# A decoder layer on one core: early context loads, and routers of two tiles in the two halves of the array

## The chip, the core and the metric

The kernel runs on one core of a Trainium2 chip. The core has TensorE (matmuls, PE in the profile; PEld is its loading of weights), VectorE (DVE), ScalarE (ACT), GpSimd (POOL) and SyncE (SP), which here only issues DMAs. [...] The metric is device microseconds of the whole program; less is better. All data is float32.

## What is computed

One decoder layer over x of shape 32 x 64 x 512, that is 2048 tokens of 512 features, in 16 tiles of 128 tokens. Three residual steps, each on a layernorm of x:

```
x = x + attention(layernorm(x))          # 32 heads of 128, RMS norm of q and k, sequences of 64
x = x + cross_attention(layernorm(x), ctx_1024)
x = x + experts(layernorm(x))

# experts, for flat tokens of 512 features, 64 experts, the best 8
logits   = flat @ router_weight.T + router_bias
scores   = softmax(logits)
w_dense  = scores where among the 8 largest of its token, else 0
out      = flat * w_dense.sum(-1) + w_dense @ expert_bias
```

In the cross attention the attention runs over features: for a batch entry, 512 features attend to 128 context features over the 64 positions; a skip product with a 64 x 64 matrix is added.

## The kernel before

The program has two stages. The first, up to about 1360 us, makes queries, keys and values of all heads and mixes them; mixed heads go to DRAM as `mixed`. The second, the output stage, multiplies the mixed heads with the output weights and runs cross attention and experts for each tile. Both parts of the change are in the second.

**The output products.** Tiles are taken in pairs: pair k has tiles 2k and 2k + 1. `first_out` does pair 0 while the last attention units finish, `strassen_out` the pairs 1 to 7. A pair is seven products (Strassen's scheme over two tiles and two halves of the features). A product is a PSUM block `py` of 128 x 256, made in four chunks of four matmuls each (`chunks`, L879). The generator yields after each chunk, so a pair has 28 chunks. At its start `strassen_out` loads the pair's mixtures a12, a22, a11, a21 (1 MB each, L863) and the residual tiles (256 KB each, L176), and has POOL add the output bias to them (L867). VectorE makes sums of the mixtures for later products (L1051, L1053, L1058, L1065; 128 x 2048 each) and adds the products to the residual tiles.

**The tails.** When a pair is done, `start_tail` puts a generator for each of its two tiles, `after_attention`, into a list. After each chunk of the next pair, `advance` lets each tail run on if the number of chunks that it asked to wait (its `yield n`) is over. So the cross attention and the experts of pair k are issued between the chunks of pair k + 1. For an even tile, counted in chunks from its first step: layernorm and the load of its context `ct` (step 0), keys (2), scores `e` and softmax (4), transposes of the probabilities into `att` (10), mixing `py_x` and the second layernorm (13), transposes of the router's input `pt_f` and their copy `ft` (17), router `pl` (19). The odd tile does these at 1, 3, 7, 13, 16, 20 and 22.

**The router** (`experts`). Four matmuls (K = 128 features each) have the 128 tokens' features as weights and the 64 columns of the router's matrix `rwt` moving, and leave logits `pl` with tokens in partitions (L1173). VectorE then works on 128 x 64 tiles: it adds the bias (L1178), finds the 8 largest (L1180) and the negated maximum (L1182); ScalarE makes the exponentials and their sum (L1185); VectorE makes the reciprocal (L1187), marks the chosen (L1190, L1192), makes the weights `wds` (L1201) and their sum (L1203), and adds the weighted input to the residual tile (L1205). The even tile ends there and keeps its weights in one half of `wds`; the odd tile, at step 26, has TensorE transpose both tiles' weights at once (`pw`, L1212), ScalarE copy them (`wt`, L1214), and at step 28 TensorE multiply with the expert biases (`pm`, L1222) in two row halves; L1225 adds them and L1226 stores the tiles. Tiles 14 and 15 run `alone`, each by itself.

**The order of work.** TensorE's instructions run in the order in which the program text issues them, everywhere. In the output stage (after `ordered.close()`, L1549) the other engines and the DMA queues are ordered by the compiler's scheduler, each engine in one queue; it also puts in the semaphores. Buffers are by tag: a tile with the same `tag` takes one of `bufs` places in turn and waits until the last reader of that place is through. The pool `output` is opened at L1551 in the memory that the pool of the attention stage left. `ps_a`, `ps_s` and `ps_t` are PSUM pools of 3, 3 and 2 banks. The first pair's order around the change:

```
work = ctx.enter_context(tc.tile_pool(name="output", bufs=2, reuse_waits="tile"))
bo_b = work.tile([P, D], F32, tag="bo", name="bo_b", bufs=1)
load(bo_b, bo.partition_broadcast(P))
outs = {1: strassen_out(1, right, start_tail, a12)}
next(outs[1])
```

Pair 1 issues six chunks, a transpose of two small matrices, one step of the tails, and so on; its mixture a12 is loaded earlier, in `drain`. The contexts of tiles 0 and 1 are loaded at L1090 in the first step of their tails.

Of the kernel before, what the change touches and what calls it, by code (L numbers as in the profile page):

```python
# [27 lines left out]
MCTX = 128  # L28
NEXP = 64
# [12 lines left out]
def decoder_layer(  # L42
# [23 lines left out]
    nc = tc.nc  # L66
# [3 lines left out]
    small = ctx.enter_context(tc.tile_pool(name="small", bufs=4))  # L70
# [5 lines left out]
    ps_a = ctx.enter_context(tc.tile_pool(name="ps_a", bufs=3, space=bass.MemoryType.PSUM))  # L76
    ps_t = ctx.enter_context(tc.tile_pool(name="ps_t", bufs=2, space=bass.MemoryType.PSUM))
    ps_s = ctx.enter_context(tc.tile_pool(name="ps_s", bufs=3, space=bass.MemoryType.PSUM))
# [136 lines left out]
    def load(to, what):  # L215

        tc.keep_in_program_order(nc.sync.dma_start(out=to, in_=what))
# [27 lines left out]
    def fill_behind(t, what):  # L245
        if (t, what) in FILL:
            fill(FILL[t, what])
# [726 lines left out]
    def strassen_out(pair, right, done, a12=None):  # L974
# [106 lines left out]
        done(ta, xa)  # L1081
        done(tb, xb)

    def cross_attention(t, xt, apart):

        name = f"x{t}"
        ct = work.tile([P, MCTX], F32, tag="ct", name=f"ct_{t}")
        nc.sync.dma_start(out=ct, in_=ctx_flat[bass.ts(t, P), :])  # L1090
        xn = layernorm(xt, name)
        yield 1
        kv = ps_s.tile([P, 2, MCTX], F32, tag="ps", name=f"kv_{t}")
        nc.tensor.matmul(kv[:, 0, :], wqk, ct, start=True, stop=True)
        nc.tensor.matmul(kv[:, 1, :], ct, xw[:, 2, :], start=True, stop=True)

        kvs = work.tile([P, 2, MCTX], F32, tag="kvs", name=f"kvs_{t}")
        nc.scalar.copy(kvs, kv)
        fill_behind(t, "keys")
        yield apart  # L1100
        halves = [slice(b * SEQ, (b + 1) * SEQ) for b in range(2)]
        e = [ps_s.tile([P, 4, MCTX], F32, tag="ps", name=f"e{b}_{name}") for b in range(2)]
        for c in range(4):
            for b, half in enumerate(halves):
                nc.tensor.matmul(  # L1105
                    e[b][:, c, :],
                    xn[half, bass.ts(c, P)],
                    kvs[half, 0, :],
                    start=True,
                    stop=True,  # L1110
                )
        def skip():
            py = ps_a.tile([P, D], F32, tag="pa", name=f"py_{name}")
            nc.tensor.matmul(py, xw[:, 3, :], xn, start=True, stop=False, skip_group_check=True)  # L1114
            return py


        py = skip() if t == NT - 1 else None
        probs = []
        for b in range(2):  # L1120

            mx = small.tile([P, 4], F32, tag="mx4", name=f"mx{b}_{name}")
            nc.vector.tensor_reduce(mx, e[b], AX.X, ALU.max)
            neg = small.tile([P, 4], F32, tag="neg4", name=f"neg{b}_{name}")
            nc.vector.tensor_scalar(neg, mx, -(SEQ**-0.5), None, ALU.mult)
            prob = work.tile([P, 4, P], F32, tag="probx", name=f"prob{b}_{name}", bufs=3)
            sums = small.tile([P, 4], F32, tag="sums4", name=f"sums{b}_{name}")
            for c in range(4):
                nc.scalar.activation(
                    prob[:, c, :],  # L1130
                    e[b][:, c, :],
                    AF.Exp,
                    bias=neg[:, c : c + 1],
                    scale=SEQ**-0.5,
                    accum_out=sums[:, c : c + 1],
                )
            inv = small.tile([P, 4], F32, tag="inv4", name=f"inv{b}_{name}")
            nc.vector.reciprocal(inv, sums)
            nc.vector.tensor_tensor(prob, prob, _bc(inv, P), ALU.mult)
            probs.append(prob)  # L1140
        yield 5
        att = work.tile([P, 2, 4, P], F32, tag="att", name=f"att_{name}", bufs=1)
        for b in range(2):
            nc.scalar.copy(att[:, b, :, :], transposed(probs[b], f"{name}_{b}"))
        fill_behind(t, "probabilities")
        yield 2
        py = py or skip()
        for b, half in enumerate(halves):
            nc.tensor.matmul(  # L1149
                py[half, :],  # L1150
                kvs[:, 1, half],
                att[:, b, :, :].rearrange("m c n -> m (c n)"),
                start=False,
                stop=b == 1,
                skip_group_check=True,
            )
        fill_behind(t, "mixtures")
        nc.vector.tensor_tensor(xt, xt, py, ALU.add)
# [3 lines left out]
    def experts(t, xt):  # L1162
        name = f"f{t}"
        xn = layernorm(xt, name)

        yield 8 if t == NT - 2 else 3
        ft = work.tile([P, KC, P], F32, tag="ft", name=f"ft_{name}", bufs=1)
        nc.scalar.copy(ft, transposed(xn.rearrange("p (kc k) -> p kc k", k=P), name))
        fill_behind(t, "router's input")
        yield 1  # L1170
        pl = ps_s.tile([P, NEXP], F32, tag="ps", name=f"pl_{name}")
        for kc in range(KC):
            nc.tensor.matmul(  # L1173
                pl, ft[:, kc, :], rwt[:, kc, :], start=kc == 0, stop=kc == KC - 1
            )
        fill_behind(t, "router")
        lg = work.tile([P, NEXP], F32, tag="lg", name=f"lg_{name}")
        nc.vector.tensor_tensor(lg, pl, rb_b, ALU.add)  # L1178
        top = small.tile([P, 8], F32, tag="top", name=f"top_{name}")
        nc.vector.max(top, lg)  # L1180
        neg = small.tile([P, 1], F32, tag="neg", name=f"neg_{name}")
        nc.vector.tensor_scalar(neg, top[:, 0:1], -1.0, None, ALU.mult)  # L1182
        ex = work.tile([P, NEXP], F32, tag="ex", name=f"ex_{name}")
        den = small.tile([P, 1], F32, tag="den", name=f"den_{name}")
        nc.scalar.activation(ex, lg, AF.Exp, bias=neg, accum_out=den)  # L1185
        inv = small.tile([P, 1], F32, tag="inv1", name=f"inv1_{name}")
        nc.vector.reciprocal(inv, den)  # L1187

        rest = work.tile([P, NEXP], F32, tag="rest", name=f"rest_{name}")
        nc.vector.match_replace(rest, top, lg, -3e38)  # L1190
        chosen = work.tile([P, NEXP], F32, tag="chosen", name=f"chosen_{name}")
        nc.vector.tensor_tensor(chosen, lg, rest, ALU.not_equal)  # L1192

        alone = t >= NT - 2
        side = 0 if alone else t % 2
        if side:
            wds, other = chosen_by.pop(t - 1)
        else:
            wds = work.tile([P, 2, NEXP], F32, tag="wds", name=f"wds_{name}")
        wd = wds[:, side, :]  # L1200
        nc.vector.scalar_tensor_tensor(wd, ex, inv, chosen, ALU.mult, ALU.mult)  # L1201
        ws = small.tile([P, 1], F32, tag="ws", name=f"ws_{name}")
        nc.vector.tensor_reduce(ws, wd, AX.X, ALU.add)  # L1203

        nc.vector.scalar_tensor_tensor(xt, xn, ws, xt, ALU.mult, ALU.add)  # L1205
        if not alone and not side:
            chosen_by[t] = wds, xt
            return
        yield 3
        n = NEXP if alone else 2 * NEXP  # L1210
        pw = ps_t.tile([P, P], F32, tag="pt", name=f"pw_{name}")
        nc.tensor.transpose(pw[0:n, :], wds.rearrange("p a e -> p (a e)")[:, 0:n], ident)  # L1212
        wt = work.tile([P, P], F32, tag="wt", name=f"wt_{name}")
        nc.scalar.copy(wt[0:n, :], pw[0:n, :])  # L1214
        fill_behind(t, "weights")
        yield 1

        both = [(t, xt)] if alone else [(t - 1, other), (t, xt)]
        pms = [ps_a.tile([P, D], F32, tag="pa", name=f"pm{i}_{name}") for i in range(len(both))]
        for i, pm in enumerate(pms):  # L1220
            rows = slice(i * NEXP, (i + 1) * NEXP)
            nc.tensor.matmul(pm, wt[rows, :], eb_sb[rows, :], start=True, stop=True)  # L1222
        fill_behind(t, "experts")
        for (at, it), pm in zip(both, pms):
            nc.vector.tensor_tensor(it, it, pm, ALU.add)  # L1225
            nc.sync.dma_start(out=out_flat[bass.ts(at, P), :], in_=it)  # L1226

# [323 lines left out]
    work = ctx.enter_context(tc.tile_pool(name="output", bufs=2, reuse_waits="tile"))  # L1551
    bo_b = work.tile([P, D], F32, tag="bo", name="bo_b", bufs=1)
    load(bo_b, bo.partition_broadcast(P))
    outs = {1: strassen_out(1, right, start_tail, a12)}
    next(outs[1])

# [88 lines left out]
```

## Time and profile before

| | |
|---|---|
| median of 3 runs | 1869.87 us (1869.63 to 1870.72) |
| the profiled execution | 1869.75 us |
| its span, first to last instruction | 1868.0 us |
| granted TensorE clock | 0.999 |
| instructions | 40676 |

Where the time of the changed parts stands in the groups of the output stage:

| line | what | count | busy us | mean ns |
|---|---|---|---|---|
| L1173 | router matmuls, 128x64 moving | 128 records | 16.2 | 270 |
| L1105 | scores of the cross attention, 64*128, 128x128 | 256 records | 19.1 | 285 |
| L1149 | mixing of the cross attention, 128*64, 128x512 | 64 records | 17.3 | 618 |
| L1094 | keys, 128x128 | 32 records | 6.2 | 276 |
| L1205 | residual of the experts, 128x512 | 16 | 12.0 | 748 |
| L1185 | exponentials of the router, 128x64 | 16 | 5.6 | 348 |

How to read it: a float32 matmul shows as two records, a transpose as one. Records overlap, so a group's cost on TensorE is read from start to start in a timeline or from the chain of waits, not from its busy time. `128*64` ahead of a form is the part of the array that is used: 128 rows (the contraction) by 64 columns; two matmuls in different halves can be in the array together. In a timeline the columns are start, duration (both us), engine, line, operation, output and inputs, count, and in brackets the idle time before and what ended it.

### The profile page before, as it was taken

The page shows a single profiled execution, that of the slowest core. Times are in us where ns is not written, and L with a number is a line of the kernel's source. Part 1 is how long each engine was busy: PE and PEld are TensorE (multiplying, and loading weights), DVE is VectorE, ACT ScalarE, POOL GpSimd, SP SyncE. Part 2 cuts the span into 40 slices and gives each one's busy share as a digit, 9 for nine tenths or more (in the row PEclk, how much of TensorE's full clock was granted, in tenths as well). Part 3 has the DMA queues.
Part 4 walks back from the last instruction along what each step waited for, and adds up shares of the span by engine and source line. Part 5 has one row for each costly group of instructions (what it writes and reads, how often), then busy time and mean ns, then how long its engine had stood idle before and what let it go on. Part 6 is the DMA issues. An engine that isn't in the chain of part 4 may idle for free.

```text
span 1868.0 us, 40676 instructions
## 1 busy us (share of the span) xinstructions
PE 1850.4 (99%) x16914; PEld 1616.9 (87%) x16914; DVE 1245.1 (67%) x2110; ACT 653.6 (35%) x1577; POOL 1014.7 (54%) x852
## 2 busy tenths in 40 slices
PE   9999999999999999999999999999999999999999
PEld 8888998898899888898889988988888888788876
DVE  6877777777666758777667767766684445554555
ACT  2344444444433443434443343444312202221222
POOL 4866777776667639776667777766242121212120
PEclk9999999999999999999999999999999999999999
DMA  4234434433443343333343333334944231223100
GB/s 143 69 122 144 134 125 131 131 109 110 131 136 114 114 139 112 109 109 103 130 134 123 109 110 114 103 115 141 312 122 159 91 116 68 71 94 116 46 26 23
DMA packets 164650, 215.06 MB, mean 115 GB/s; under 512 B 10161, under 2 KB 135153, under 8 KB 160369
## 3 DMA queue, kind: packets, MB, share of 16 engines
q1 hardware_dynamic: 157648, 206.62, 34.2%
q10 hardware_dynamic: 6816, 5.83, 1.0%
q8 instruction: 133, 2.18, 0.5%
q14 instruction: 53, 0.43, 0.1%
HBM read 172.05 MB, written 40.37 MB: 114 GB/s over the span
## 4 chain that ended last, share of the span: by engine, by line
PE 88%; DVE 4%; DMA 3%; POOL 3%; ACT 1%; issue 1%; SPq 0%; ACTq 0%; POOLq 0%; DVEq 0%
PE p_w L685 32%; PE py L879 17%; PE va L417 11%; PE vb L417 8%; PE o L622 3%; PE s L585 3%; PE ms_w L821 3%; PE pt_p L279 1%; PE pa L475 1%; PE e_x L1105 1%; PE py_x L1149 1%; PE pt_x L279 1%; POOL w L120 1%; PE pl_f L1173 1%; PE py_x L1114 1%; PE pb L475 1%
## 5 line engine op out<-in xcount | busy, mean ns | idle before, releaser
L685 PE MATMUL p_w<-x,w 128*128 128x256 f32 x2940 | 721.1, 382 | 2.5 <-DVE qk L696 1.7
L685 PEld LDWEIGHTS p_w<-x,w 128*128 128x128 f32 x2940 | 521.4, 190 | 59.3 <-DVE qk L696 1.2
L417 PEld LDWEIGHTS va<-w,x 128*128 128x128 f32 x2048 | 268.6, 192 | 13.0
L696 DVE TENSOR_TENSOR qk<-p_w,qk 128x512 f32<-128x512 f32 x360 | 213.1, 599 | 94.6 <-PE p_w L685 92.3
L433 ACT COPY v<-va 128x256 f32<-128x256 f32 x256 | 96.2, 376 | 497.5 <-PE va L417 497.5
L417 PE MATMUL va<-w,x 128*128 128x128 f32 x2048 | 269.9, 275 | 0.0
L709 DVE TENSOR_TENSOR qk<-p_w,qk 128x512 f32<-128x512 f32 x360 | 220.5, 620 | 46.5 <-PE p_w L685 43.1
L120 POOL TENSOR_TENSOR w<-w 128x768 f32<-128x768 f32 x126 | 249.7, 1993 | 2.4
L572 POOL TENSOR_TENSOR qk<-qk,rs 128x512 f32<-128x512 f32 x128 | 173.0, 1352 | 111.8 <-DMA rs<-row_w 99.4
L295 POOL TENSOR_TENSOR prob<-prob,inv 128x512 f32<-128x512 f32 x64 | 79.2, 1237 | 281.5 <-DVE inv L294 278.3
L879 PE MATMUL py<-wo,a 128*128 128x256 f32 x992 | 227.2, 382 | 0.0
L386 ACT ACTIVATE sq<-qk 128x512 f32<-128x512 f32 x256 | 161.4, 631 | 183.6 <-DVE qk L709 64.4
L879 PEld LDWEIGHTS py<-wo,a 128*128 128x128 f32 x992 | 184.1, 190 | 32.9 <-issue 8.6
L417 PEld LDWEIGHTS vb<-w,x 128*128 128x128 f32 x1536 | 201.3, 192 | 9.7
L417 PE MATMUL vb<-w,x 128*128 128x128 f32 x1536 | 202.4, 275 | 0.0
L574 DVE SCALAR_TENSOR_TENSOR qk<-qk,gqk,rs 128x512 f32<-128x512 f32 x128 | 164.7, 1287 | 3.8 <-DMA rs<-row_w 3.5
L879 PE MATMUL py<-wo_t,a 128*128 128x256 f32 x672 | 155.1, 382 | 0.0
L879 PEld LDWEIGHTS py<-wo_t,a 128*128 128x128 f32 x672 | 124.3, 190 | 18.2 <-issue 1.6
L1003 POOL TENSOR_TENSOR x<-x,p 128x256 f32<-128x256 f32 x42 | 42.9, 1043 | 166.7 <-ACT p L1056 72.2
L437 DVE TENSOR_TENSOR v<-vb,v 128x256 f32<-128x256 f32 x192 | 80.9, 421 | 57.0 <-ACT v L433 28.8
L765 POOL TENSOR_TENSOR qk<-qk 128x256 f32<-128x256 f32 x120 | 102.8, 857 | 10.5 <-DVE qk L709 5.8
L287 DVE TENSOR_REDUCE mx<-s 128x8 f32<-128x512 f32 x64 | 44.1, 689 | 85.4 <-PE s L585 85.3
(197 smaller groups left out, 2253.7 us busy)
## 6 DMA issues: line engine op xcount, KB each, us to landing
rs<-row_w SPq DMA_DIRECT2D x120, 512.0 KB
mixed<-ot SPq DMA_DIRECT2D x64, 512.0 KB
a<-mixed SPq DMA_DIRECT2D x32, 1024.0 KB
w<-in_wq_dram SPq DMA_DIRECT2D x64, 256.0 KB
w<-in_wk_dram SPq DMA_DIRECT2D x62, 256.0 KB
w<-in_wv_dram SPq DMA_DIRECT2D x62, 256.0 KB
x<-in_x_dram SPq DMA_DIRECT2D x20, 256.0 KB
rs<-row SPq DMA_DIRECT2D x8, 512.0 KB
```

The lines of the kernel that those rows point to most:

```text
L120: on.tensor_tensor(*(it.rearrange("p c j d -> p (c j) d") for it in (out, a, b)), ALU.subtract)
L386: nc.scalar.activation(sq, of, AF.Square)
L417: nc.tensor.matmul(to[:, j, :], left[i][:, c, j, :], right[i][:, c, 2, :], start=first and j == 0 and c == 0, stop=c == 1, skip_group_chec ...
L433: nc.scalar.copy(self.v[h, ab], what)
L437: nc.vector.tensor_tensor(it, what, it, ALU.add)
L572: nc.gpsimd.tensor_tensor(k, k, rk, ALU.mult)
L574: lambda: nc.vector.scalar_tensor_tensor(q, q, gqk, rq, ALU.mult, ALU.mult)
L685: nc.tensor.matmul(bank[:, s, :], self.w.inner[o][i], inner_x[self.half, o][i], start=first and s == 0, stop=True, skip_group_check=True,)
L696: nc.vector.tensor_tensor(to(t, j), bank, add(t, j), ALU.add)
L709: nc.vector.tensor_tensor(to(t, j), bank, to(t, j), ALU.add)
L765: on.tensor_tensor(to, to, what, ALU.add)
L879: nc.tensor.matmul(py, a[:, g, :], b[g // KH][:, g % KH, :], start=n == 0 and g == 0, stop=n == last and g == NHG - 1,)
```

## The change

Two parts. The contexts of tiles 0 and 1 get their tiles and loads in front of `strassen_out(1, ...)`, so ahead of the loads of pair 1's mixtures; `cross_attention` takes them from the dictionary `contexts`, and loads the context itself for all other tiles, as before.

For tiles 0 to 13 the router runs once for both tiles of a pair, at the odd tile's step. The even tile copies its transposed input into one half of `fts` (in the buffer tagged `att`, 128 x 1024) and returns; the odd tile fills the other half. The router's matrix (128 x 64) is now the weights and the 128 tokens move; even and odd tile write partitions 0 to 63 and 64 to 127 of one bank, `plt`, in turn for each of the four parts of the contraction. ScalarE copies this to SBUF (`lgt`); one chunk later TensorE transposes it, so that tokens are in partitions again, and VectorE adds the bias for both tiles in one operation. The operations from the maximum to the residual then run for the two tiles one after the other in the program text. The wait ahead of `pw` goes from `yield 3` to `yield 0` and `yield 2`, so `pw` and `pm` stay in their steps (26 and 28). Tiles 14 and 15 keep the router of before, with their input in the `att` buffer.

```diff
+    contexts = {}
+
+    def context(t):
         ct = work.tile([P, MCTX], F32, tag="ct", name=f"ct_{t}")
         nc.sync.dma_start(out=ct, in_=ctx_flat[bass.ts(t, P), :])
+        return ct
...
+        ct = contexts.pop(t, None) or context(t)
...
-        ft = work.tile([P, KC, P], F32, tag="ft", name=f"ft_{name}", bufs=1)
+        alone = t >= NT - 2
+        if alone or t % 2 == 0:
+            fts = work.tile([P, 2, KC, P], F32, tag="att", name=f"ft_{name}", bufs=1)
+        else:
+            fts, x_a, xn_a = chosen_by.pop(t - 1)
+        ft = fts[:, 0 if alone else t % 2, :, :]
         nc.scalar.copy(ft, transposed(xn.rearrange("p (kc k) -> p kc k", k=P), name))
         fill_behind(t, "router's input")
         yield 1
-        pl = ps_s.tile([P, NEXP], F32, tag="ps", name=f"pl_{name}")
-        for kc in range(KC):
-            nc.tensor.matmul(
-                pl, ft[:, kc, :], rwt[:, kc, :], start=kc == 0, stop=kc == KC - 1
-            )
-        fill_behind(t, "router")
...
+        elif t % 2 == 0:
+            chosen_by[t] = fts, xt, xn
+            return
         else:
+            tiles = [(t - 1, x_a, xn_a), (t, xt, xn)]
+
+            plt = ps_s.tile([P, P], F32, tag="ps", name=f"plt_{name}")
+            for kc in range(KC):
+                for side in range(2):
+                    nc.tensor.matmul(
+                        plt[side * NEXP : (side + 1) * NEXP, :],
+                        rwt[:, kc, :],
+                        fts[:, side, kc, :],
+                        start=kc == 0,
+                        stop=kc == KC - 1,
+                    )
+            lgt = work.tile([P, P], F32, tag="wt", name=f"lgt_{name}")
+            nc.scalar.copy(lgt, plt)
+            yield 0
+            pl = ps_s.tile([P, 2, NEXP], F32, tag="ps", name=f"pl_{name}")
+            nc.tensor.transpose(pl.rearrange("p a e -> p (a e)"), lgt, ident)
+        n = len(tiles)
+        lgs = work.tile([P, n, NEXP], F32, tag="lg", name=f"lg_{name}")
+        nc.vector.tensor_tensor(
+            lgs, pl, rb_b.unsqueeze(1).to_broadcast([P, n, NEXP]), ALU.add
+        )
+        wds = work.tile([P, n, NEXP], F32, tag="wds", name=f"wds_{name}")
+        for side, (at, x_, xn_) in enumerate(tiles):
+            lg = lgs[:, side, :]
...
+            wd = wds[:, side, :]
+            nc.vector.scalar_tensor_tensor(wd, ex, inv, chosen, ALU.mult, ALU.mult)
...
+            nc.vector.scalar_tensor_tensor(x_, xn_, ws, x_, ALU.mult, ALU.add)
+        yield 3 if alone else 2
+        n *= NEXP
...
     load(bo_b, bo.partition_broadcast(P))
+
+    contexts.update({t: context(t) for t in range(2)})
     outs = {1: strassen_out(1, right, start_tail, a12)}
```

More of the change, by code (lines that the diff above doesn't have):

```diff
@@ L1082, in strassen_out @@
         done(tb, xb)
+    contexts = {}
+    def context(t):
+        ct = work.tile([P, MCTX], F32, tag="ct", name=f"ct_{t}")
+        nc.sync.dma_start(out=ct, in_=ctx_flat[bass.ts(t, P), :])
+        return ct
     def cross_attention(t, xt, apart):
         name = f"x{t}"
-        ct = work.tile([P, MCTX], F32, tag="ct", name=f"ct_{t}")
-        nc.sync.dma_start(out=ct, in_=ctx_flat[bass.ts(t, P), :])
+        ct = contexts.pop(t, None) or context(t)
         xn = layernorm(xt, name)
@@ L1170, in experts @@
         yield 1
-        pl = ps_s.tile([P, NEXP], F32, tag="ps", name=f"pl_{name}")
-        for kc in range(KC):
-            nc.tensor.matmul(
-                pl, ft[:, kc, :], rwt[:, kc, :], start=kc == 0, stop=kc == KC - 1
-            )
-        fill_behind(t, "router")
[L1177 to L1197, printed above, removed]
-        else:
-            wds = work.tile([P, 2, NEXP], F32, tag="wds", name=f"wds_{name}")
-        wd = wds[:, side, :]
-        nc.vector.scalar_tensor_tensor(wd, ex, inv, chosen, ALU.mult, ALU.mult)
@@ L1202, in experts @@
[L1202 to L1210, printed above, removed]
+        if alone:
+            tiles = [(t, xt, xn)]
+            pl = ps_s.tile([P, 1, NEXP], F32, tag="ps", name=f"pl_{name}")
+            for kc in range(KC):
+                nc.tensor.matmul(
+                    pl[:, 0, :], ft[:, kc, :], rwt[:, kc, :], start=kc == 0, stop=kc == KC - 1
+                )
+            fill_behind(t, "router")
+        elif t % 2 == 0:
+            chosen_by[t] = fts, xt, xn
+            return
+        else:
+            tiles = [(t - 1, x_a, xn_a), (t, xt, xn)]
+            plt = ps_s.tile([P, P], F32, tag="ps", name=f"plt_{name}")
+            for kc in range(KC):
+                for side in range(2):
+                    nc.tensor.matmul(
+                        plt[side * NEXP : (side + 1) * NEXP, :],
[9 more added lines that the diff above has]
+            nc.tensor.transpose(pl.rearrange("p a e -> p (a e)"), lgt, ident)
@@ new lines, in experts @@
+        n = len(tiles)
+        lgs = work.tile([P, n, NEXP], F32, tag="lg", name=f"lg_{name}")
+        nc.vector.tensor_tensor(
+            lgs, pl, rb_b.unsqueeze(1).to_broadcast([P, n, NEXP]), ALU.add
+        )
+        wds = work.tile([P, n, NEXP], F32, tag="wds", name=f"wds_{name}")
+        for side, (at, x_, xn_) in enumerate(tiles):
+            lg = lgs[:, side, :]
+            top = small.tile([P, 8], F32, tag="top", name=f"top{side}_{name}")
+            nc.vector.max(top, lg)
+            neg = small.tile([P, 1], F32, tag="neg", name=f"neg{side}_{name}")
+            nc.vector.tensor_scalar(neg, top[:, 0:1], -1.0, None, ALU.mult)
+            ex = work.tile([P, NEXP], F32, tag="ex", name=f"ex{side}_{name}")
+            den = small.tile([P, 1], F32, tag="den", name=f"den{side}_{name}")
+            nc.scalar.activation(ex, lg, AF.Exp, bias=neg, accum_out=den)
+            inv = small.tile([P, 1], F32, tag="inv1", name=f"inv1{side}_{name}")
+            nc.vector.reciprocal(inv, den)
+            rest = work.tile([P, NEXP], F32, tag="rest", name=f"rest{side}_{name}")
+            nc.vector.match_replace(rest, top, lg, -3e38)
+            chosen = work.tile([P, NEXP], F32, tag="chosen", name=f"chosen{side}_{name}")
+            nc.vector.tensor_tensor(chosen, lg, rest, ALU.not_equal)
+            wd = wds[:, side, :]
+            nc.vector.scalar_tensor_tensor(wd, ex, inv, chosen, ALU.mult, ALU.mult)
+            ws = small.tile([P, 1], F32, tag="ws", name=f"ws{side}_{name}")
+            nc.vector.tensor_reduce(ws, wd, AX.X, ALU.add)
+            nc.vector.scalar_tensor_tensor(x_, xn_, ws, x_, ALU.mult, ALU.add)
@@ L1216, in experts @@
         yield 1
-        both = [(t, xt)] if alone else [(t - 1, other), (t, xt)]
-        pms = [ps_a.tile([P, D], F32, tag="pa", name=f"pm{i}_{name}") for i in range(len(both))]
+        pms = [ps_a.tile([P, D], F32, tag="pa", name=f"pm{i}_{name}") for i in range(len(tiles))]
         for i, pm in enumerate(pms):
@@ L1223, in experts @@
         fill_behind(t, "experts")
-        for (at, it), pm in zip(both, pms):
+        for (at, it, _), pm in zip(tiles, pms):
             nc.vector.tensor_tensor(it, it, pm, ALU.add)
```

## The prediction

> **What bounds the kernel now.** I read the page's busy times and its chain first, then the waits of TensorE over the last 490 us (the changed lines run only there), then the timelines of TensorE and VectorE around those waits.
>
> ```profile
> PE 1850.4 (99%) x16914; PEld 1616.9 (87%) x16914; DVE 1245.1 (67%) x2110; ACT 653.6 (35%) x1577; POOL 1014.7 (54%) x852
> ...
> PE 88%; DVE 4%; DMA 3%; POOL 3%; ACT 1%; issue 1%; SPq 0%; ACTq 0%; POOLq 0%; DVEq 0%
> ```
>
> TensorE is busy throughout and is 88% of the chain. Its order is written by hand, so in the output stage each piece taken out of its queue, or each of its waits removed, moves everything behind it. A measurement of this kernel can tell some 0.2% from no change, 3.74 us. The waits of TensorE from 1380 us on:
>
> ```profile
> PE kv L1094 <- DMA ct<-in_ctx_dram: 2.2, 1, 2.2
> PE pm_f L1222 <- DVE x L1225: 0.8, 1, 0.8
> PE e_x L1105 <- ACT prob_x L1129: 0.6, 1, 0.6
> ```
>
> Only the first, once in the kernel, is of the size of a microsecond or two: the keys of tile 0 wait for their context. The timelines of TensorE and of SyncE's queue show it:
>
> ```profile
> 1414.09 1.89 PE L879 MATMUL py<-wo_t,a 128*128 128x256 f32 x8
> 1418.13 0.46 PE L1094 MATMUL kv<-ct,wqk 128*128 128x128 f32 x2 [2.15 <-DMA ct<-in_ctx_dram]
> ...
> 1396.91 0.62 SPq L217 DMA_DIRECT2D bo_b<-in_bo_dram  x1
> 1397.58 9.51 SPq L863 DMA_DIRECT2D a<-mixed  x3
> 1407.18 0.38 SPq L176 DMA_DIRECT2D x<-in_x_dram  x1
> 1407.61 4.16 SPq L1090 DMA_DIRECT2D ct<-in_ctx_dram  x2
> ```
>
> The contexts stand behind three mixture loads and a residual; the first needed 10.38 us to land. Now the router, from the chain of waits in a later pair (a record pair is one f32 matmul, so x8 of `py` is four):
>
> ```profile
> 1580.61 0.84 PE pl_f L1173 x8
> 1581.45 6.96 PE py L879 x32
> ...
> 1599.08 0.22 PE kv L1095 x2
> 1599.31 1.73 PE py L879 x8
> 1601.03 1.09 PE e_x L1105 x16
> 1602.13 5.38 PE py L879 x24
> ```
>
> Four `py` matmuls undisturbed take 1.73 us, so 32 records take 6.91 and 24 take 5.18. A router costs 0.84 and 0.05 behind it: 0.89. The scores `e_x`, 8 matmuls in halves of the array, cost 1.09 and 0.20 behind them.
>
> **Contexts.** Two loads of 64 KB move ahead of the mixture loads; the two old places vanish, so no DMA is added. The gain is the wait: the keys go from 1418.13 to 1415.98, **-2.15 us**, if nothing else is late next. Moved past are, on SyncE's queue, the mixtures a22, a11, a21 and a residual. (1) a22 is read without a wait at 1408.46. The share of the DMA engines falls from 0.97 in 1402-1404 to 0.35 in 1404-1406, so it was through near 1405. The 128 KB ahead of it at the 240 GB/s moved in 1398-1400 are 0.55 us, and two issues of 0.33 to 0.78 us overlap that: over 1.5 us are left. (2) a11 is read next, now from 1416.5. SyncE's waits show a `ct` issue held for 3.0 us by a mixture load until 1411.45, so that one, I take it a11, has landed 5 us before. (3) The residual lands at 1417.87; VectorE waits for it and then works without a break (L1050, L1051, L1053, maxima, L1058, L1065) until the second probability of tile 0 at 1433.47. TensorE transposes that at 1435.9, then 2.15 earlier, at 1433.8: covered by 0.3 us. With that cover gone the gain shrinks by as much as the residual is later. Bounds: -2.15, and, if all of it reappears at that transpose, 0. I take -2.15, since cover is left at each place.
>
> POOL issues none of these loads; its bias addition of the residual still waits for the same DMA.
>
> **Router, TensorE.** Seven pairs change; tiles 14 and 15 keep their four matmuls. Removed per pair: 2 x 0.89 = 1.78 us. Added: 8 matmuls with 64 columns of weights and 128 tokens moving, alternately in the two halves, and one transpose. The trace has no such form with K = 128 and 128 moving columns. A whole-array matmul with 128 moving columns costs 0.22 (`kv`), and a 64-column one (`pl`) 0.21: the tokens moving are free by themselves. If the halves did not overlap, 8 x 0.22 + 0.20 = 1.96. The nearest rows say they do: `e_x` has the same 8 matmuls of 128 columns, in row halves, at 1.09 + 0.20; the mixing in L1149 (128*64, two matmuls of 512, so as many columns) takes 1.01 + 0.19; and `s` has exactly the column halves with alternating weights:
>
> ```profile
> 1381.94 1.15 PE L585 MATMUL s<-qk 128*64 128x64 f32 x32
> 1383.02 1.16 PE L622 MATMUL o<-probt,v 64*64 64x64 f32 x64
> ```
>
> 16 matmuls in 1.08 us from start to start, with twice as many weight loads as here. I take `e_x`'s 1.29. The transpose is like `pw`: 0.11. Per pair 1.78 - 1.40 = 0.38, seven pairs **-2.7 us**. Bounds: with L1149's 1.01 and no cost behind it 0.66 a pair, -4.6; without overlap -0.29 a pair, +2.0.
>
> [...]
>
> **Router, the rest.** ScalarE gains one copy a pair, 128x128 from PSUM, 0.27 us like `wt`, after which one chunk of `py` (1.73 us) runs before the transpose needs it; ScalarE is idle there for over 4 us (it waits that long for `neg_f`). The input tile shares its buffer with `att`; the last reader, the mixing of the odd tile, is one chunk ahead of the even tile's copy. Cost nothing.
>
> VectorE loses one addition (0.22) a pair, but the even tile's chain moves behind the odd tile's, and both start one chunk later with TensorE's `pw` still in the same step. What is queued behind a late `pw` is all of TensorE. Before:
>
> ```profile
> 1581.49 0.22 DVE L1178 TENSOR_TENSOR lg_f<-pl_f,rb_b 128x64 f32<-128x64 f32 x1 [3.80 <-PE pl_f L1173]
> 1582.87 0.28 DVE L1201 SCALAR_TENSOR_TENSOR wds_f<-ex_f,inv_f,chosen_f 128x64 f32<-128x64 f32 x1
> 1583.32 0.41 DVE L1072 TENSOR_TENSOR p<-py,p 128x256 f32<-128x256 f32 x1
> 1588.25 0.27 PE L1212 MATMUL pw_f<-ident,wds_f 128*128 128x128 f32 x1
> ```
>
> Weights were ready at 1583.15 and asked for at 1588.25: 5.1 us of slack. After, counted from the end T of the router matmuls: the transpose ends at T + 1.93 + 0.11 = 2.04, `pw` stands at 2.04 + 3 x 1.73 = 7.2. VectorE: start 2.24; the wide addition 0.33 (between 0.22 for 64 and 0.42 for 256 columns, with its gap); L1072 and L1073 0.8; two chains from maximum to weights 2 x 1.40 (1581.75 to 1583.15); of the sum and residual update of the even tile, if they come between, 0.26 + 0.67. Weights ready at 7.1, or at 6.2 if the order keeps the updates for last. Slack 0.1 to 1.0: no wait in the steady pairs. Tiles 0 and 1 have layernorms of the next pair beside them, but also 0.45 of keys on TensorE; tiles 12 and 13 have tile 14's (0.69 + 0.18 + 0.55), and I put **+0.2** for them.
>
> **Sum.** -2.15 - 2.7 + 0.2 = -4.65. The profiled execution took 1869.75 (span 1868.0 and 1.75 around it): 1865.1. The median is 0.12 above that execution; forecast **1865.2**.
>
> **Rivals.**
> - *Contexts gain nothing* (the residual or a22 late, VectorE's row the new bound): the router's 2.5 stays, 1867.3. For: only 0.3 us of cover. Against: no load is added. 12%.
> - *The halves don't overlap*, or the change doesn't make TensorE faster: -2.15 + 2.0 + 0.2, 1869.8. Against: three rows with overlap. 6%.
> [...]
> - *A short wait at `pw`*, 0.2 to 0.5 a pair: -4.65 + 7 x 0.35, 1867.5. For: slack 0.1 in one order. 8%.
> - *Slower: POOL's additions hold the two chains up.* L1072 releases three additions of POOL (L1003, 2.53 us from 1583.82); before, the odd chain was over by then, now both chains run beside them. L269 took 0.94 and 1.48 us beside POOL in two places (1815.38, 1788.88) and 0.55 elsewhere. If two operations of a chain lose 0.93 each, weights are ready at 7.1 + 1.86 and TensorE, which takes 0.15 to follow, stands 1.9 a pair; seven pairs +13.3: 1878.4. It decides from 0.66 us of waiting a pair, where the whole -4.65 is gone. For: the same engine pair, the same moment. Against: L1205 beside the same additions took 0.74, as it does without them. 8%.
>
> My forecast has 60%, alone between 1864.0 and 1866.6; it lies above the 3.74 us bound in 51 of its 60 parts. Faster then is 51 + 6 + 2 of the two near ones = 0.59; slower 0.08; same 0.33. The range takes in the first rivals and ends at the no-overlap case: 1863.8 to 1869.8; outside are the slower case, the one without switching cost and a little more.
>
> **What would show it.** `kv` without a DMA wait near 1416; `pt_x` of tile 0 without a wait for `prob_x`; `plt` at 1.0 to 1.1 us a pair with a `py` behind it 0.2 longer; no wait of `pw` on `wds`; `lgt` inside one chunk. Wrong it would be with a wait of TensorE of over 0.3 us on `wds`, on `lgt` or on a mixture, or with `plt` near 1.7.

## The result, and the profile after

Over 16 runs each, the kernel before took 1870.3 us (1866.9 to 1873.4) and the changed one 1866.2 us (1863.4 to 1871.9): a ratio of 0.9979, 95% interval 0.9971 to 0.9988. The forecast was 1865.2. The profiled execution took 1864.01 us, with a span of 1862.2; it is 2.2 us below its median, so it shows more than the change gave in the median. The interval leaves out 1, so the change is faster; the 0.2% that the prediction took as the least it could tell from no change (0.9980) lies inside the interval, so whether the gain passes that bound stays open.

On the page, TensorE's busy time is 6.6 us less (1850.4 before), and the chain is TensorE's to 90%:

```profile
PE 1843.8 (99%) x16921; PEld 1607.8 (86%) x16921; DVE 1244.2 (67%) x2103; ACT 653.7 (35%) x1584; POOL 1012.6 (54%) x852
...
PE 90%; DVE 4%; POOL 3%; DMA 2%; issue 1%; ACT 0%; SPq 0%; POOLq 0%; DVEq 0%; ACTq 0%
```

The waits of TensorE from 1370 us on (us in total, times, longest):

```profile
PE pm_f L1252 <- DVE x L1255: 0.8, 1, 0.8
PE e_x L1111 <- ACT prob_x L1135: 0.6, 1, 0.6
PE pm_f L1252 <- ACT wt_f L1245: 0.3, 1, 0.3
```

The wait of `kv` on its context is gone, and no wait on `wds`, `lgt` or a mixture has come. The timelines of TensorE and of SyncE's queue around the place:

```profile
1413.86 1.89 PE L879 MATMUL py<-wo_t,a 128*128 128x256 f32 x8
1415.59 0.38 PE L1100 MATMUL kv<-ct,wqk 128*128 128x128 f32 x2
...
1397.35 2.15 SPq L1088 DMA_DIRECT2D ct<-in_ctx_dram  x2
1400.85 5.02 SPq L863 DMA_DIRECT2D a<-mixed  x3
1407.17 0.33 SPq L176 DMA_DIRECT2D x<-in_x_dram  x1
```

Then the router, in the chain of waits of a steady pair (start, us, what):

```profile
1572.74 3.46 PE py L879 x16
1576.20 1.02 PE plt_f L1200 x16
1577.22 1.92 PE py L879 x8
1579.15 0.11 PE pl_f L1211
1579.26 5.18 PE py L879 x24
```

Eight matmuls in halves take 1.02 us, the four `py` behind them 1.92 instead of 1.73, the transpose 0.11: 1.32 us where two routers took 1.78.

**A measure for all runs.** The first product of pair 1 (32 records of `py`) started at 1401.56 before and at 1401.33 after; among the profiles below it lies between 1401.33 and 1407.32, in code that none of them changes. So I count from there to the end of the span and call that the stage: 466.44 us before, 460.87 after, 5.57 less. The first key stands 14.26 us behind that product wherever it doesn't wait; what it stands later than that is its delay: 1418.13 - 1401.56 - 14.26 = 2.31 us before, 0 after.

### The profile page after: what moved, and what is told of

It reads as the page before. It is cut to its first block, busy times and chain, and to the rows that moved or that the text cites. A ratio compares the mean times of both kernels' runs of the same rounds, so it can differ in the third digit from the quotient of the medians.

```text
span 1862.2 us, 40700 instructions
## 1 busy us (share of the span) xinstructions
PE 1843.8 (99%) x16921; PEld 1607.8 (86%) x16921; DVE 1244.2 (67%) x2103; ACT 653.7 (35%) x1584; POOL 1012.6 (54%) x852
## 4 chain that ended last, share of the span: by engine, by line
PE 90%; DVE 4%; POOL 3%; DMA 2%; issue 1%; ACT 0%; SPq 0%; POOLq 0%; DVEq 0%; ACTq 0%
PE p_w L685 32%; PE py L879 19%; PE va L417 11%; PE vb L417 8%; PE o L622 3%; PE s L585 3%; PE ms_w L821 3%; PE pt_p L279 1%; PE pa L475 1%; PE e_x L1111 1%; PE py_x L1155 1%; PE pt_x L279 1%; POOL w L120 1%; PE py_x L1120 1%; PE pb L475 1%
## 5 line engine op out<-in xcount | busy, mean ns | idle before, releaser
L574 DVE SCALAR_TENSOR_TENSOR qk<-qk,gqk,rs 128x512 f32<-128x512 f32 x128 | 169.9, 1327 | 4.1 <-DMA rs<-row_w 3.5
L1003 POOL TENSOR_TENSOR x<-x,p 128x256 f32<-128x256 f32 x42 | 40.8, 992 | 163.7 <-ACT p L1056 72.5
L765 POOL TENSOR_TENSOR qk<-qk 128x256 f32<-128x256 f32 x120 | 102.9, 858 | 10.5 <-DVE qk L709 5.8
```

The source lines that it names most:

```text
L574: lambda: nc.vector.scalar_tensor_tensor(q, q, gqk, rq, ALU.mult, ALU.mult)
L765: on.tensor_tensor(to, to, what, ALU.add)
```

## The experiments

| kernel | median us (runs) | ratio to before, 95% | stage us | delay of the first key us |
|---|---|---|---|---|
| before, first profile | 1870.3 (16) | | 466.44 | 2.31 |
| after | 1866.2 (16) | 0.9979 (0.9971 to 0.9988) | 460.87 | 0 |
| contexts_only | 1870.19 (11) | 0.9992 (0.9982 to 1.0001) | 464.05 | 0 |
| router_only | 1867.48 (11) | 0.9981 (0.9973 to 0.9990) | 461.09 | 0 |
| halves_in_sequence | 1869.29 (11) | 0.9996 (0.9987 to 1.0005) | 464.28 | 0 |
| tokens_as_weights | 1870.10 (11) | 0.9996 (0.9987 to 1.0005) | 464.07 | 0 |
| pw_one_earlier | 1871.06 (10) | 1.0003 (0.9993 to 1.0014) | 465.84 | 0 |
| ctx_on_act | 1866.12 (12) | 0.9978 (0.9969 to 0.9987) | 461.14 | 0 |
| ctx_behind_mixtures | 1866.82 (10) | 0.9981 (0.9969 to 0.9992) | 462.75 | 1.74 |
| best | 1864.75 (9) | 0.9970 (0.9960 to 0.9981) | 459.15 | 0 |
| before_look1, 2, 3 | 1868.08, 1869.77, 1871.25 (1 each) | | 464.82, 466.19, 464.60 | 0.70, 0.41, 0.47 |
| router_look | 1866.77 (1) | | 462.24 | 1.24 |

Each ratio is to the kernel before as it ran beside that kernel: a median of 1870.30 us beside the change, 1870.40 beside the next four rows and 1870.17 beside the four from pw_one_earlier to best. The last two rows are one execution for each profile.

### Each part alone

**contexts_only**: the kernel before with the lines of the diff that load the contexts early, and its own routers.

> The contexts of tiles 0 and 1 are loaded early, the router is that of before. Measured by the output stage, from the first matmul of pair 1's first product to the end of the span (466.4 us before, 460.9 after the whole change). My theory: the wait of the first keys (2.15 us) goes and nothing takes its place, 464.2, total time 2.2 us less than before. The rival, that the residual's landing takes over at the transposes of tile 0: 465.5 to 466.4.

The stage is 464.05, 2.39 less than in the first profile of before, and no key waits. That is the theory's number. But the median is only 0.2 us below that of before beside it (1870.40), by the ratio 1.5 us with an interval that holds zero.

**router_only**: the change without its early loads.

```diff
-    contexts.update({t: context(t) for t in range(2)})
     outs = {1: strassen_out(1, right, start_tail, a12)}
```

> The router of the change, contexts loaded in the old place. My theory: the wait of 2.15 us of the first keys is there again, and the router saves 0.45 us in each of seven pairs; output stage 466.4 - 3.2 = 463.2. With the contexts-only run the savings add up to the 5.6 us of the change. The rival, that the two parts share a cause (a queue order that either part alone changes): the two savings don't add up, off by over 0.5 us.

A miss: 461.09, and the key has no wait, though the contexts stand where they stood before. The timeline of this kernel's TensorE:

```profile
1417.07 0.43 PE L1100 MATMUL kv<-ct,wqk 128*128 128x128 f32 x2
```

So the 2.31 us of delay were either taken away by the routers' change, or they are not in every execution. Four more profiles, further below, decide between the two.

### Why the router is cheaper

**halves_in_sequence**: the same eight matmuls, but all four of one half before those of the other.

```diff
-            for kc in range(KC):
-                for side in range(2):
+            for side in range(2):
+                for kc in range(KC):
```

> As after the change, but the four matmuls of the even tile come first and then the four of the odd tile, so that successive matmuls stand in the same half of the array. My theory, that the gain is the overlap of two matmuls in different halves: 8 x 0.21 + 0.1 = 1.8 us from start to start instead of 1.02 a pair, output stage +5 to +6 over the change (466.2). The rival, that a 64-column weight load alone makes them cheap, with or without overlap: 1.0 to 1.1 us, no change of the stage (460.9).

Its chain of waits in a steady pair:

```profile
1583.16 1.51 PE plt_f L1200 x16
1584.67 1.93 PE py L879 x8
1586.60 0.11 PE pl_f L1211
```

1.51 + 0.20 + 0.11 = 1.82 us, 0.50 more than with the halves in turn, seven times 3.5; the stage is 3.41 longer. The same work in another order loses the whole gain. The 1.51 is less than the 1.8 expected, a miss in size, and the starts of the single records in the two traces show why. Within a half the records start 0.109 us apart in both kernels, so 0.22 for a matmul holds. After the change the two halves' records start in couples, 7 ns apart. In this run the second half's first record starts 0.49 us behind the first half's (1583.59 and 1583.10), while three of the first half's eight records are still to come (by their spacing; the last starts at 1583.91). So the halves overlap here too, but only in part, and the 0.49 is the whole difference between 1.51 and 1.02: overlap between the halves is the gain.

**tokens_as_weights**: both tiles' routers at the odd tile's step, with one addition and the same chains on VectorE, but matmuls as before, so no `lgt` and no transpose.

```diff
-            plt = ps_s.tile([P, P], F32, tag="ps", name=f"plt_{name}")
-            for kc in range(KC):
-                for side in range(2):
+            pl = ps_s.tile([P, 2, NEXP], F32, tag="ps", name=f"pl_{name}")
+            for side in range(2):
+                for kc in range(KC):
                     nc.tensor.matmul(
-                        plt[side * NEXP : (side + 1) * NEXP, :],
-                        rwt[:, kc, :],
+                        pl[:, side, :],
                         fts[:, side, kc, :],
+                        rwt[:, kc, :],
...
-            lgt = work.tile([P, P], F32, tag="wt", name=f"lgt_{name}")
-            nc.scalar.copy(lgt, plt)
...
-            nc.tensor.transpose(pl.rearrange("p a e -> p (a e)"), lgt, ident)
```

> As after the change, with early contexts and both tiles' chains at the odd tile's step, but the router's matmuls in the old form: the tokens are the weights and 64 columns move, 2 x 4 matmuls in the whole array, with no copy and no second transpose. My theory: the eight cost 8 x 0.21 + 0.05 = 1.73 us a pair, as before; only the contexts' 2.2 us stay, output stage 464.2. The rival, that joining the two tiles' chains or dropping the even tile's step is what saves: 461 to 462.

Its chain of waits:

```profile
1580.11 1.73 PE pl_f L1200 x16
1581.84 6.96 PE py L879 x32
```

1.73 and 0.05 behind it, 1.78 as before; 0.46 a pair over the change, and the stage is 3.20 longer (7 x 0.46 = 3.2). Putting the pair together gains nothing by itself; the form of the matmuls is worth the 3.2 us.

### How near `pw` is to a wait

**pw_one_earlier**: `pw` and `pm` one chunk earlier.

```diff
-        yield 3 if alone else 2
+        yield 3 if alone else 1
```

> As after the change, but the transpose of the weights stands one chunk of four matmuls (1.73 us) earlier. In the changed kernel the weights of a steady pair are ready 5.55 us after the router's matmuls, and the transpose stands at 7.1. My theory: at 5.4 it waits 0.2 to 0.4 us a pair, 1.5 to 3 us in all. By the order that I predicted, chains one after the other (ready at 7.1), it would wait 1.8 a pair, 12 us in all.

The stage is 5.0 us longer than after: over the 1.5 to 3 of the theory, under the 12 of the other order. Its waits of TensorE from 1400 us on:

```profile
PE e_x L1111 <- DVE mv_x L256: 2.2, 1, 2.2
PE pw_f L1243 <- DVE wds_f L1235: 1.0, 1, 1.0
```

`pw` waits for its weights 1.0 us for tiles 12 and 13. In the five steady pairs it waits 0.3 us each, which this view doesn't list (the `py` ahead of it is through at about 1585.52 by the price of its 16 records, 3.46, the weights are ready at 1585.68 and `pw` starts at 1585.82); with the two timelines set side by side each of these pairs is 0.33 longer than after, 1.7 in all. This part is the theory's 0.2 to 0.4 a pair. The wait of the scores `e_x`, the largest, I had not foreseen. In POOL's timeline two additions of the bias to the next residual tiles now stand ahead of the layernorm of the cross attention that the scores need (by the chain of waits; the view above names a VectorE step beside it), and wait for their loads:

```profile
1782.80 1.27 POOL L867 TENSOR_TENSOR x<-x,bo_b 128x512 f32<-128x512 f32 x1 [13.35 <-DMA x<-in_x_dram]
1784.46 1.26 POOL L867 TENSOR_TENSOR x<-x,bo_b 128x512 f32<-128x512 f32 x1 [0.39 <-DMA x<-in_x_dram]
1785.68 0.22 POOL L259 TENSOR_SCALAR rs_x<-mv_x 128x1 f32<-128x1 f32 x1
```

After the change as made, that order is the other way round: POOL's L259 at 1779.08, its L867 at 1783.47. And behind the 2.2 us of idle time 24 records of `py` took 7.13 instead of 5.45: the granted clock was 0.50 for 3.4 us there. Set side by side, the two timelines of TensorE give the 5.0 us (4.9 by the unrounded spans) in these steps: 1.7 for the steady pairs, 2.3 for tile 12's scores, 1.7 for the clock and 0.8 over the pair of tiles 12 and 13, less 0.4 in the first pair and 1.1 at tile 13's scores, which have no wait here.

### Where the contexts must stand

**ctx_on_act**: the early loads, issued by ScalarE's queue and not by SyncE's (`context(t, nc.scalar)`).

> As after the change, but the two early contexts are issued on ScalarE's queue instead of SyncE's. In the changed kernel the first mixture of pair 1 was issued at 1400.85, 3.3 us later than before, behind the contexts. My theory: it goes back to 1397.4, the keys have their contexts all the same, and the stage is as long as after the change (460.9), because TensorE did not wait for that mixture. The rival, that the delay of the mixture is paid somewhere in pair 1: 460 or less.

461.14, no wait on a context; 0.2 of the 0.3 us above the change is `e_x` of tile 13, which waits 0.8 and not 0.6 for the exponentials. In this run it makes no difference to TensorE which queue issues them.

**ctx_behind_mixtures**: early, but behind the three mixture loads and ahead of the residuals.

```diff
+        if pair == 1:
+            contexts.update({t: context(t) for t in range(2)})
         xa, xb = load_residual(ta), load_residual(tb)
...
-    contexts.update({t: context(t) for t in range(2)})
```

> As after the change, but the contexts are issued behind the four mixture loads of pair 1 and ahead of the residuals. My theory, that the place ahead of the mixtures is what counts: the first keys wait again, 1 to 2.2 us, stage 462 to 463.1. The rival, that being ahead of the residual is enough: no wait, 460.9.

The timeline of its TensorE:

```profile
1419.35 0.46 PE L1102 MATMUL kv<-ct,wqk 128*128 128x128 f32 x2 [1.57 <-DMA ct<-in_ctx_dram]
```

The delay is back at 1.74, and 462.75 - 1.74 = 461.0. Being ahead of the residual is not enough; what the contexts must pass is the mixtures.

### Is the wait in every execution?

Four more profiles, of the kernel before three times and of router_only once, unchanged. Below, look 1 to 3 are the second to fourth profile of before.

> The kernel before, unchanged, profiled a second time. In its first profile the first key product of pair 1 waited 2.15 us for its context, and SyncE's issue of the second tile's first mixture had waited 7.2 us for the small xw loads of another queue. With the old routers alone put right (router_only) that issue waited 4.0 us and the key product not at all. Theory A: the wait is not a property of the kernel but of the execution, between 0 and 2.2 us, set by how long SyncE's queue is held up by the xw loads; then the output stage is between 464.2 us (no wait) and 466.4 us (2.2 us), and its length minus the wait on the context comes out at 464.2 within 0.4. Theory B: the wait is fixed at 2.0 to 2.3 us in the kernel before, and it was the routers' change that took it away in router_only; then the stage is 466.2 to 466.7 with a wait of 2.0 to 2.3 in every look.

> The kernel before once more. Theory A: a wait on the context anywhere from 0 to 2.2 us, and a stage of 464.2 us plus that wait. Theory B: 2.0 to 2.3 us and 466.2 to 466.7 us again.

> The kernel before a fourth time, for the spread. Theory A: the wait on the context differs between the looks by over 0.5 us, and follows the time at which SyncE's queue issued the context. Theory B: the looks agree within 0.3 us.

> The changed routers alone, with the contexts where they were, profiled a second time (the first profile: stage 461.09 us, no wait on the context). Theory A: a stage of 461.0 us plus whatever the context's wait is this time, 0 to 2.2 us, so 461.0 to 463.2. Theory B, the routers' change removes the wait: 461.1 us and no wait again.

TensorE's timelines, one line each of look 1, look 2, look 3 and router_look:

```profile
1416.44 0.46 PE L1094 MATMUL kv<-ct,wqk 128*128 128x128 f32 x2 [0.55 <-DMA ct<-in_ctx_dram]
```
```profile
1416.38 0.46 PE L1094 MATMUL kv<-ct,wqk 128*128 128x128 f32 x2 [0.25 <-DMA ct<-in_ctx_dram]
```
```profile
1419.63 0.46 PE L1094 MATMUL kv<-ct,wqk 128*128 128x128 f32 x2 [0.31 <-DMA ct<-in_ctx_dram]
```
```profile
1418.26 0.46 PE L1100 MATMUL kv<-ct,wqk 128*128 128x128 f32 x2 [1.08 <-DMA ct<-in_ctx_dram]
```

The same program waited 2.15, 0.55, 0.25 and 0.31 us; router_only waited 0 and 1.08. Theory B, a fixed wait that the routers took away, has fallen. Less the delay, the stage of before is 464.13, 464.12 and 464.13 in three profiles (the first, look 1 and look 3), that of router_only 461.09 and 461.00: apart from the delay, these repeat to 0.1 us.

Look 2 is the exception: 466.19 - 0.41 = 465.78, against 464.2 within 0.4 expected. Its place can be found by setting the two timelines of TensorE side by side. Up to the experts' second product of tile 1 (`pm`, L1222), which waits 0.78 us for VectorE in both, they run alike to 0.1 us. Then look 1:

```profile
1477.67 1.12 PE L1222 MATMUL pm_f<-eb_sb,wt_f 64*128 64x512 f32 x2 [0.78 <-DVE x L1225]
1478.72 3.72 PE L879 MATMUL py<-wo_t,a 128*128 128x256 f32 x16
```

and look 2:

```profile
1477.61 1.12 PE L1222 MATMUL pm_f<-eb_sb,wt_f 64*128 64x512 f32 x2 [0.78 <-DVE x L1225]
1478.66 5.41 PE L879 MATMUL py<-wo_t,a 128*128 128x256 f32 x16
```

The same 16 records took 1.69 us longer, and 465.78 - 1.69 = 464.09. The windows of look 2 show the granted clock there (the third number from the end):

```profile
1478.00:1479.00 1.00, 1.00 (x3) 0.33 (x2) 0.97 (x3) 0.24 (x2) 0.00 (x0) 0.94 0.58 219
1479.00:1480.00 1.00, 1.00 (x4) 0.75 (x3) 0.78 (x2) 0.00 (x0) 0.00 (x0) 0.50 0.12 43
```

What sets the size of the context's delay is only partly shown. I had expected it to follow the time of the context's issue; that is a miss: behind the first product the first context was issued at 6.05 us in the first profile of before and between 6.13 and 6.48 in the later profiles and in router_only. What differs is the time from there to the key that it released (10.5 us in the first profile, 8.3 in look 2), and with it how long ahead of the context the second tile's first mixture (1 MB) had gone out: 1.56 us ahead in the first profile, where SyncE's queue had stood 7.2 us for the small `xw` loads (the releaser that the profile infers), and 4.94 in router_only, where it had stood 4.0. ctx_behind_mixtures fits this: the queue stood 7.1 us and the delay was 1.74. Between these ends the order isn't strict (3.43 us ahead with a delay of 0.41, 3.51 with 1.24), so the rest stays open.

### A version that is faster than both

**best**: the change, one yield between the two products `pm` of tile 1, and the scores of tile 13 one chunk later.

```diff
+            if t == 1 and i == 0:
+                yield 0
...
-        yield 5
+        yield 4 if t == NT - 3 else 5
...
-        yield from cross_attention(t, xt, 3 if second else 1)
+        yield from cross_attention(t, xt, 4 if t == NT - 3 else 3 if second else 1)
```

> As after the change, with the two largest waits left taken out by order alone: the two expert products of tiles 0 and 1 stand one chunk apart (0.78 us of waiting), and the scores of tile 13 one chunk later (0.64 us). My theory: both waits go and nothing else changes, stage 460.9 - 1.4 = 459.5. The rival, that VectorE only moves the waits: 460.5 to 461.

The stage is 459.15, 1.72 less than after, where the theory had 1.4 from the two waits. By the two timelines side by side, 0.65 comes from the products `pm` and 1.12 from tile 13's scores: after the change their first matmul ran at 1787.16 and the other seven only at 1788.28, so more than the 0.64 us of waiting was lost there. From pair 1's first product on, TensorE waits for these alone:

```profile
PE pm_f L1252 <- ACT wt_f L1245: 0.3, 1, 0.3
PE pl_f L1187 <- ACT ft_f L1180: 0.2, 1, 0.2
PE pt_x L279 <- DVE prob_x L1145: 0.2, 1, 0.2
```

Its median of 1864.75 is the lowest, below that of before in the times too; against the change the intervals of the ratios overlap, and the 1.7 us are shown by the stage, not by the times.

## Why the prediction held, and where its sizes were off

The direction, the two sources and the place of each were right. The sizes were not all.

**Contexts, -2.15.** The mechanism is shown: contexts_only and the change have no wait, ctx_behind_mixtures has it again (1.57). The step that failed is "I take -2.15, since cover is left at each place". The cover was not the weak point; the wait itself was. Its delay in four profiles of before is 2.31, 0.70, 0.41 and 0.47, 0.97 on the mean, and the first profile held the largest. That one execution was read as the kernel's property. The rival that the contexts gain nothing was nearer in size than its 12% suggest, though for a reason that it didn't name. The times say no more: router_only has a ratio of 0.9981 and the whole change 0.9979, so what the early contexts give in the median is not shown apart from noise.

**The covers.** (1) a22 was issued at 1400.85, not some half a microsecond but 3.3 us later than before (1397.58), since SyncE also waited 1.3 us for a `mixed` store; still the product that reads it started at 1408.24 without a wait. (2) a11 went out at 1402.46, earlier than before (1406.05). (3) The residual landed at 1415.83, 2.0 us earlier, so VectorE's chain moved with TensorE (it was not "without a break": it waited 1.51 us for ScalarE's exponentials at 1427.03, and 1.50 after), and the transpose at 1432.87 had no wait. The 0.3 us of cover that worried me was counted against a load that moved too.

**Router on TensorE, -2.7.** Mis-sized: 1.32 us a pair, not 1.40, so 0.46 saved and not 0.38; contexts_only and the change differ by 464.05 - 460.87 = 3.18. The right row was L1149 (1.01, with 0.19 behind), which has column halves as the new router has; `e_x` (1.09), which I took, has row halves. The rival "no overlap" is out: 1.02 and not 1.76. The 6 in the sum of the chances of faster stands for a case without switching cost, whose price no run shows: the eight matmuls took 1.02, and the `py` behind them 0.19 longer.

**VectorE, +0.2.** Not paid. The transpose ended at 1579.26 and the chains ran so:

```profile
1579.86 0.28 DVE L1214 TENSOR_TENSOR lg_f<-pl_f,rb_b 128x128 f32<-128x128 f32 x1
1580.17 0.35 DVE L1221 MAX8 top_f<-lg_f 128x8 f32<-128x64 f32 x2
...
1582.43 0.27 DVE L1235 SCALAR_TENSOR_TENSOR wds_f<-ex_f,inv_f,chosen_f 128x64 f32<-128x64 f32 x1
1582.62 0.74 DVE L1239 SCALAR_TENSOR_TENSOR x<-xn_f,ws_f,x 128x512 f32<-128x512 f32 x1
```

Both tiles' maxima stand together, so the two chains are interleaved, and the updates L1239 come last. The weights were ready at 1582.70, 5.5 us behind the router's end, not 6.2 or 7.1; `pw` started at 1584.28. The slack is 1.6 us, 1.4 with the 0.14 that TensorE takes to follow, which pw_one_earlier bears out: one chunk (1.73) earlier, the steady pairs wait 0.3 us. For tiles 12 and 13 the weights were ready at 1822.68 and `pw` started at 1823.86.

**The slower rival.** POOL's three L1003 additions ran right beside the chains, as the rival had it, and one operation was longer, the second tile's `chosen`. A steady pair, and below it the pair of tiles 12 and 13, which has no L1003 beside it:

```profile
1579.69 2.10 POOL L1003 TENSOR_TENSOR x<-x,p 128x256 f32<-128x256 f32 x3 [12.26 <-DVE p L1072]
1580.95 0.91 DVE L1233 TENSOR_TENSOR chosen_f<-lg_f,rest_f 128x64 f32<-128x64 f32 x2
1820.30 0.35 DVE L1233 TENSOR_TENSOR chosen_f<-lg_f,rest_f 128x64 f32<-128x64 f32 x2
```

All 16 of these operations, before (L1192) and after (L1233), with their shortest, median and longest in ns:

```profile
L1192 DVE TENSOR_TENSOR chosen_f<-lg_f,rest_f x16: 206/224/225, 1459.2 to 1860.6; 128x64 f32<-128x64 f32 x16
L1233 DVE TENSOR_TENSOR chosen_f<-lg_f,rest_f x16: 216/226/761, 1465.0 to 1854.9; 128x64 f32<-128x64 f32 x16
```

In each of the five steady pairs the second one took 0.76 us; it began 0.05 us after the third L1003 and ended 0.08 after it, so that 0.68 of it ran beside that addition. The other eleven took 0.22 or 0.23, and of these the first one of each steady pair ran beside L1003 all the time. So a loss like the rival's came, at one operation and 0.54 us a pair, not at two of 0.93 each, and it is part of the 5.5 us; that POOL is what makes it is not shown. The slack of 1.4 us that was left behind it kept it from TensorE. In pw_one_earlier that slack is gone, and by estimate the 0.3 us of its steady pairs would not be there without these 0.54. Apart from that, an order of POOL's queue held up TensorE there, at L867.

**The sum.** From 1865.2, with the contexts' mean (+1.2), the router's size (-0.5), the 0.2 not paid and the larger set's median of before (+0.4): 1866.1, against 1866.2 measured. That 1865.2 came within 1 us is in part luck, since 0.7 of errors one way was set against 1.6 the other way; the contexts' share among them rests on the mean of four profiles with delays from 0.41 to 2.31.

## What to carry to other kernels

The wait on the context was 2.15, 0.55, 0.25 and 0.31 us in four profiles of one program: profile the same program several times before the whole length of a wait on a DMA is counted as a gain, and measure from a landmark behind the noisy part to the end. To price a matmul form, take the row with the same split of the array (here 1.01 us in column halves and 1.09 in row halves, for 1.02 measured in column halves), and issue the halves in turn: the order alone was worth the 3.4 us. When TensorE's work moves by a chunk, look at what the queues of POOL and VectorE put ahead of what it needs next (the largest piece of pw_one_earlier came from there), and compare the times of each VectorE operation where POOL works beside it (0.76 and 0.23 us here) and where it doesn't (0.22 or 0.23).

## What was not expected of the hardware

- **Half clock behind a short wait.** Before and after end at a granted clock of 0.50 (from 1867.6 and 1861.9 us on), and eight profiles, before among them, have a mean of 0.83 to 0.88 between 10 and 20 us. Apart from these, three show a stretch of 3.4 us at 0.50, which cost 1.66 to 1.69 us: look 2 (1479 to 1482) behind a wait of 0.78, pw_one_earlier (1789 to 1792) behind one of 2.23, halves_in_sequence (134 to 137) at two of 1.35 and 0.82. The length of the wait doesn't decide it here: the 0.78 wait stands in 13 of the profiles and was followed by half clock once, and waits of 2.15 (before) and 1.57 (ctx_behind_mixtures) were not. What does set it off is not shown. A lower clock goes with a longer time: of 65 executions of before, the 20 with a granted clock of 0.998 or less took 1872.1 us on the mean, the other 45 took 1870.2.
- **Order within the array.** Eight float32 matmuls with 128 x 64 weights and 128 columns moving took 1.02 us with the halves in turn and 1.51 half by half, where the second half began 0.49 us later; with tokens as weights and 64 columns moving, whole array, 1.73.
- **One load, 8.3 to 10.5 us.** In four profiles of the same program the same 64 KB load released its key product that long after its issue, with the issue at the same place to 0.5 us.
- **VectorE beside POOL.** In every steady pair after the change, one 128x64 comparison (L1233) took 0.76 us with one of POOL's L1003 additions beside 0.68 of it, and the comparison just ahead of it took 0.23 with L1003 beside all of it; those with no L1003 beside them took 0.22 or 0.23. What makes the one longer is not shown. The prediction had a loss beside POOL as a rival, with other operations and a larger price.
